# A four-column exponential moved later in ScalarE's order, in an attention and feed-forward kernel

## The chip, the cores and the metric

The kernel runs on one core of a Trainium2 chip. The metric is the device time of one launch in microseconds; smaller is better.

## What is computed

The input x has 8 batches of 1024 rows and 256 columns, in fp32. Cut to what matters, the reference is:

```python
q, k, v = x @ Wq.T + bq, x @ Wk.T + bk, x @ Wv.T + bv      # split into 16 heads of 16
q = softmax(q, axis=-1)                                    # over a head's 16 columns
k = softmax(k, axis=-2)                                    # over the batch's 1024 rows
state = einsum('bhnd,bhne->bhde', k, v)                    # 16 x 16 per head
out = einsum('bhnd,bhde->bhne', q, state)                  # back to (8, 1024, 256)
x = layernorm(x + layernorm(out) @ Wo.T + bo)

h = gelu(layernorm(x) @ ternary(w1).T + b1)                # 1024 hidden columns
x = layernorm(x + layernorm(h) @ ternary(w2).T + b2)
```

The keys' softmax is over all rows of a batch, and the kernel treats a batch in two blocks. Each block takes its own maximum of the keys; at the end the two blocks have to be weighed against each other with the exponential of (block's maximum minus the larger maximum). That weight is the subject of the change.

## The kernel before

**Blocks.** The 8 batches of 1024 rows are 16 blocks of 512 rows (`blocks`, two for each batch: g = 0 and g = 1; so odd blocks have g = 1). A block is 4 tiles of 128 rows.

**The order is written out by hand.** `ORDER` is a table of strings. The main loop takes i from 0 to 20 and reads one string for each i: "early" for the first four, "mid" for 4 to 15, and strings of their own for the five at the end. Each word of a string is a piece, and `piece(what, i)` issues it. One pass of a string works on several blocks at once: queries and keys of block i, attention of an earlier block, and the feed-forward part (`H`, `A`, `B`) of a still earlier one. Each engine executes its own instructions in the order in which the pieces issue them and waits on semaphores for the others.

**Work that is dealt out in between.** VectorE's small work (norms, statistics, residual sums) is written as generators. They lie in the queues `soon`, `behind` and `later`, and `more(n)` takes n steps from them; the words `m`, `m1` to `m8` are calls of it.

**The pieces beside the change:**

- `k0`, `k1`, `kb`, `ke`: the keys. `keys_exp` is two exponentials of 128x512 on ScalarE (L383), with the block's maximum as bias; the block's sum goes to `z[b]`.
- `bs`: `blocks_sum(b)`, in odd blocks only. VectorE takes the maximum of the two blocks' maxima (L460, `m`), after one step of dealt-out work subtracts it (L463, `e`, 128x4), and ScalarE takes the exponential in place (L466).
- `te0`, `te2`: `turn_keys`, TensorE transposes of the keys, copied by ScalarE to `ek` (L400).
- `a`: `attend`, matmuls to `po` (L545), copied by ScalarE to `o` and `y` (L550, L551); VectorE takes statistics of `o` (L555, L557).
- `qe`, `qs`: the queries' exponential on ScalarE (L428, 128x1024), their sums and reciprocals on VectorE (L433, L435), and the product on GpSimd (L436).
- `bw`: `blocks_weights(b)`, in odd blocks only: four small VectorE instructions (L471, L473, L475, L477) that turn `e` into the two weights. The first of them needs the exponential.
- `cr`: in odd blocks the weights are used: `first_block` on ScalarE (L482) and `second_block` on VectorE (L489). Then a DMA adds the row `crow` to x (L991).
- `A`, `B`: `product`, the second matmul of the feed-forward part (L726) into PSUM `pf`; when a half is done ScalarE copies it to `zs[i]` (L739, called z in the profile), a tile with one buffer. `rest(i)` reads it on VectorE (L798, L803) to update x.
- `en`: `enter`, a GpSimd product to `h0` (L614) and a DMA (L617). `ti0`, `ti1`: its transposes (`pth`), copied by ScalarE and VectorE (L635, L636).
- `sh`, `sq`: `sum_halves` and `sum_squares`: a DMA that adds two halves (L699), and TensorE's transposes of the sum (`psq`, L711).

The name z stands for two things in the profile: `zs[i]` of L739 and L798, and the small sums of L471 and L473.

Of the kernel before, what the change touches and what calls it, by code (L numbers as in the profile page):

```python
# [11 lines left out]
AF = mybir.ActivationFunctionType  # L12
# [13 lines left out]
def attn_ffn_postln_kernel(  # L26
# [11 lines left out]
    nc = tc.nc  # L38
    B, N, C = x.shape
# [283 lines left out]
    es, mb, z, mx, a0, aT, sT, sm = {}, {}, {}, {}, {}, {}, {}, {}  # L323
# [133 lines left out]
    def blocks_sum(b):  # L457

        m = small.tile([P, KC], F32, tag="m", name=f"m_{b}")
        nc.vector.tensor_tensor(m, mb[b][:, 0, :], mb[b][:, 1, :], ALU.max)  # L460
        e = small.tile([P, NB, KC], F32, tag="e", name=f"e_{b}")
        more(1)
        nc.vector.tensor_tensor(  # L463
            e, mb[b], m.unsqueeze(1).to_broadcast([P, NB, KC]), ALU.subtract
        )
        nc.scalar.activation(e, e, AF.Exp)  # L466
        es[b] = e, m

    def blocks_weights(b):
        e, m = es[b]  # L470
        nc.vector.tensor_tensor(z[b], z[b], e, ALU.mult)  # L471
        more(1)
        nc.vector.tensor_tensor(m, z[b][:, 0, :], z[b][:, 1, :], ALU.add)  # L473
        more(1)
        nc.vector.reciprocal(m, m)  # L475
        more(1)
        nc.vector.tensor_tensor(e, e, m.unsqueeze(1).to_broadcast([P, NB, KC]), ALU.mult)  # L477
# [127 lines left out]
    h0, hT, ph, u, sq, sqs, sums, sn, pf, mv, rs, sc, ms, zs = ({} for _ in range(14))  # L605
# [75 lines left out]
    def lower(n):  # L681

        i, j = n // HC, n % HC
        if upper_on_vector(n):
            nc.vector.tensor_scalar(u[n][:, 0, :], ph[n], gm[:, j : j + 1], None, ALU.mult)
        nc.vector.scalar_tensor_tensor(  # L686
            u[n][:, 1, :], ph[n], gm[:, j : j + 1], u[n][:, 0, :].bitcast(F32),
            ALU.mult, ALU.subtract,
        )
        if j % 2 == 1 and 1 < j < (HC if i < len(blocks) - 1 else HC - 2):  # L690
            nc.gpsimd.dma_start(sums[i], sq[i], accum_op=ALU.add)  # L691
# [166 lines left out]
    def more(n):  # L858

        for _ in range(n):  # L860
            done = False
            for queue in (soon, behind, later):
                while queue and not done:
                    steps, wait = queue[0]
                    if wait > 0:
                        break
                    wait = next(steps, soon)
                    if wait is soon:
                        queue.pop(0)
                        continue  # L870
                    queue[0][1] = wait or 0
                    done = True
                if done:
                    break
            passed()
# [6 lines left out]
    def apply(n):  # L882

        for _ in range(n):
            if applies:
                _, x_t, sh, rs = applies.pop(0)
                nc.scalar.activation(x_t, x_t, AF.Identity, bias=sh, scale=rs)
# [6 lines left out]
    ORDER = {  # L894
        "early": """
            tx0/ph m3 m q0 m3 q2 m2 st0/ph m1 qm k0 st1/tp m2 p p k1 p st2/ph tq0/pf kb m2 st3/tp
            m tq1/w ke bs a/pf m4 m2 a/w te0/pf te2/ph m m1 p m p p p en m3 tx1/w m4 m4 x0 qe m
            bw qs a/w m6 a/w ti0/ph x1 m4 m2 cr ti1/ph m p m
        """,
        "mid": """  # L900
            H m6 H m q0 q2 m1 m2 m3 m st0/tp qm m6 H st1/tp sq/w H p m k0 p k1 p kb p m3 H H A m8
            A A st2/w m1 H A tq0/tp H m3 A st3/w A ke p tx0 A bs m m4 m2 a/ph A m4 m a/w tq1/ph
            a/w te0 p B te2/w qe p tx1/w p B B en B bw qs x0 ti1/ph p m4 m a/w x1 m4 B cr m1 m3
            ti0/ph B m2 m3 B m m2 p p B sh
        """,
        "16": """
# [23 lines left out]
    def turn(what, n, parts=1):  # L930

        k = count[what]
        count[what] += k < n * parts
        return (k // parts, k % parts) if k < n * parts else None
# [3 lines left out]
    def piece(what, i):  # L938
        NBL, CHUNKS = len(blocks), len(blocks) * HC
        real = i < NBL  # L940
        b, g = i // NB, i % NB
        state = g == 0 and 0 < b <= B
        if what == "H":
            one = turn("H", CHUNKS)
            if one:
                assert count["ti"] >= (one[0] // HC + 1) * KC
                hidden(one[0])
                if low:
                    lower(low.pop())
                low.append(one[0])  # L950
        elif low:
            lower(low.pop())
        if what in ("A", "B"):
            one = turn(what, CHUNKS)
            if one:
                product(one[0], "AB".index(what))
        elif what[0] == "m":
            more(int(what[1:] or 4))
            next(prep, None)
        elif what == "p":  # L960
            apply(1)
        elif what in ("q0", "q2") and real:
            queries(i, int(what[1]))
        elif what == "qm" and real:
            queries_max(i)
        elif what == "qe" and real:
            queries_exp(i)
        elif what == "qs" and real:
            queries_sum(i)
        elif what in ("k0", "k1") and real:  # L970
            keys(i, int(what[1]))
        elif what == "kb" and real:
            keys_bias(i)
        elif what == "ke" and real:
            keys_exp(i)
        elif what == "bs" and real and g == 1:
            blocks_sum(b)
        elif what == "bw" and real and g == 1:
            blocks_weights(b)
        elif what in ("te0", "te2") and real:  # L980
            turn_keys(i, int(what[2]))
        elif what in ("x0", "x1") and real:
            keys_x(i, int(what[1]))
        elif what == "cr" and real:
            if g == 0:
                a0[b] = big.tile([P, KC, C], F32, tag="a0", bufs=2, name=f"a0_{b}")
                nc.scalar.copy(a0[b], pa[i])
            else:
                first_block(b)
                second_block(b)  # L990
            nc.gpsimd.dma_start(  # L991
                x_of(i), crow.unsqueeze(1).to_broadcast([P, G, C]), accum_op=ALU.add
            )
        elif what in ("tx0", "tx1"):
            turn_x(i + 1, int(what[2]))
        elif what[:2] == "tq" and i > 0:
            one = turn("tq", NBL, KC)
            if one:
                turn_queries(*one)
        elif what == "st0" and state:  # L1000
            state_turn(b - 1)
        elif what == "st1" and state:
            state_values(b - 1)
        elif what in ("st2", "st3") and state:
            state_out(b - 1, int(what[2]) - 2)
        elif what == "a" and i > 1:
            one = turn("a", NBL, G)
            if one:
                assert count["tq"] >= (one[0] + 1) * KC
                attend(*one)  # L1010
                if one[1] == G - 1:
                    (behind if one[0] > NBL - 3 else later).append([norm(one[0]), 0])
        elif what == "en" and i > 2:
            one = turn("en", NBL)
            if one:
                while one[0] not in normed:
                    more(1)
                while any(a[0] <= one[0] for a in applies):
                    apply(1)
                enter(one[0])  # L1020
        elif what[:2] == "ti" and i > 2:
            one = turn("ti", NBL, KC)
            if one:
                n = one[0]
                assert count["en"] > n and count["H"] >= (n if n < NBL - 2 else 0) * HC
                turn_input(*one)
        elif what == "sh" and i > 3:
            one = turn("sh", NBL)
            if one:
                n = one[0]  # L1030
                assert count["H"] - len(low) >= n * HC + (HC if n < NBL - 1 else HC - 1)
                sum_halves(n)
        elif what == "sr" and i > last:
            if turn("sr", 1):
                assert count["sh"] == NBL and count["H"] - len(low) == CHUNKS
                add_squares(NBL - 1, sqs[CHUNKS - 1])
        elif what == "sq" and i > 4:
            one = turn("sq", NBL)
            if one:
                n = one[0]  # L1040
                assert count["sh"] > n and (n < NBL - 1 or count["sr"])
                sum_squares(n)
                if n < NBL - 1:
                    assert count["B"] >= (n + 1) * HC
                    behind.append([rest(n, (0, G)), 0])
# [3 lines left out]
    for i in range(last + 5):  # L1049
        names = {last + k: str(16 + k) for k in range(5)}  # L1050
        for what in ORDER[names.get(i, "early" if i < 4 else "mid")].split():
            what, _, tag = what.partition("/")
# [48 lines left out]
```

## Time and profile before

| what | value |
|---|---|
| median of 3 runs | 682.49 us (680.82 to 683.73) |
| profiled execution, its own time | 683.59 us |
| its span | 681.9 us |
| TensorE, matmuls | 610.2 us busy, 89% |
| VectorE | 521.1 us busy, 76% |
| ScalarE | 497.9 us busy, 73% |
| GpSimd | 298.9 us busy, 44% |
| exponential L466 | 8 instructions of 205 ns |

A profile line reads: start and duration in us, engine, line of the kernel, operation, output <- input, size; in brackets the idle time of that engine just before it and who ended it. PE is TensorE, DVE is VectorE, ACT is ScalarE, POOL is GpSimd. In the table of groups a row ends with the busy time of the group, the mean duration in ns, and the idle time ahead of it with what ended it.

### The profile page before, as it was taken

Reading aid. Unit: us, or ns where it says so; the run is one execution under the profiler, and the core shown is the slowest. Engines: PE = TensorE matmul, PEld = TensorE weight load, DVE = VectorE, ACT = ScalarE, POOL = GpSimd, SP = SyncE. Lnnn points to the kernel's source line nnn. Section 1 sums busy time; section 2 is a strip of 40 time slices with the busy share of each in tenths; the row PEclk is TensorE's granted clock in tenths of the full one; section 3 lists DMA queues with packets and bytes.
Section 4 is the critical chain, followed back from the end, with each engine's and each line's share of the span. In section 5 each row is a group of like instructions: output and inputs, shape, how many; then the busy total and the mean of one; then the engine's idle time right before and its main releaser. Section 6 shows DMA issues by size and latency. Waiting matters only on the chain.

```text
span 681.9 us, 9515 instructions
## 1 busy us (share of the span) xinstructions
PE 610.2 (89%) x3200; PEld 480.1 (70%) x3200; DVE 521.1 (76%) x1453; ACT 497.9 (73%) x936; POOL 298.9 (44%) x265
## 2 busy tenths in 40 slices
PE   5899989999999899999999899999999889977860
PEld 3567657877777687767778687777777677766750
DVE  1566776488978787788878887788878888867886
ACT  3544388797887879687887879697887878777820
POOL 1212443533454635544453635545444633562432
PEclk9889999999999999999999999999999999987985
DMA  8522242445464563547373653545463544365621
GB/s 295 192 31 32 31 62 51 78 75 93 66 151 63 124 108 82 114 69 154 62 163 55 126 106 87 112 70 120 74 128 47 126 74 110 62 108 125 139 62 62
DMA packets 34466, 66.31 MB, mean 97 GB/s; under 512 B 3408, under 2 KB 21840, under 8 KB 34416
## 3 DMA queue, kind: packets, MB, share of 16 engines
q0 software_dynamic: 25904, 45.49, 39.7%
q1 hardware_dynamic: 8240, 19.94, 7.8%
q8 instruction: 25, 0.41, 0.2%
q10 hardware_dynamic: 272, 0.26, 0.1%
q14 instruction: 25, 0.20, 0.1%
HBM read 11.95 MB, written 8.39 MB: 30 GB/s over the span
## 4 chain that ended last, share of the span: by engine, by line
PE 54%; DVE 22%; ACT 14%; issue 4%; DMA 3%; POOL 2%; SPq 0%; ACTq 0%; POOLq 0%; DVEq 0%
PE ph L659 10%; PE pf L726 9%; PE pk L363 8%; PE pa L452 7%; PE pq L409 7%; DVE x L798 5%; PE po L545 4%; ACT sq L649 4%; DVE x L803 4%; ACT ph L665 4%; DVE u L686 4%; DMA sums<-sums 2%; ACT u L668 2%; PE pth L631 2%; PE ptx L342 1%
## 5 line engine op out<-in xcount | busy, mean ns | idle before, releaser
L726 PE MATMUL pf<-t,u 128*128 128x258 f32 x1024 | 164.6, 299 | 20.6 <-ACT z L739 15.9
L726 PEld LDWEIGHTS pf<-t,u 128*128 128x128 f32 x1024 | 140.9, 192 | 37.1 <-ACT z L739 18.7
L659 PE MATMUL ph<-hT,t 128*128 128x512 f32 x512 | 149.9, 423 | 11.9 <-DVE u L686 7.6
L686 DVE SCALAR_TENSOR_TENSOR u<-ph,gm,u 128x512 fp32r<-128x512 f32 x128 | 95.4, 748 | 53.8 <-ACT sq L649 48.5
L659 PEld LDWEIGHTS ph<-hT,t 128*128 128x128 f32 x512 | 91.8, 192 | 39.1 <-DVE u L686 13.8
L665 ACT ACTIVATE ph<-ph,bh 128x512 f32<-128x512 f32 x128 | 85.0, 664 | 23.0 <-PE ph L659 21.2
L545 PE MATMUL po<-sm,qT 128*128 128x384 f32 x256 | 92.9, 488 | 0.0
L668 ACT ACTIVATE u<-ph,gm 128x512 fp32r<-128x512 f32 x120 | 82.5, 688 | 3.9
L436 POOL TENSOR_TENSOR q<-q,rq 128x1024 f32<-128x1024 f32 x16 | 31.0, 1940 | 101.7 <-DVE rq L435 101.7
L691 POOL DMA_DIRECT2D sums<-sq x47 | 42.6, 905 | 73.9 <-DMA sums<-sq 21.1
L649 ACT ACTIVATE sq<-ph,shift 128x512 f32<-128x512 f32 x96 | 65.3, 681 | 0.2
L452 PE MATMUL pa<-x,ek 128*128 128x256 f32 x256 | 61.5, 384 | 0.2 <-ACT ek L400 0.2
L144 POOL TENSOR_TENSOR ny_y<-nvy,mhalf 128x8 f32<-128x8 f32 x16 | 26.5, 1657 | 77.6 <-DVE nvy L584 77.6
L409 PE MATMUL pq<-wqkv_sb,xT 128*128 128x256 f32 x256 | 59.8, 387 | 0.0
L363 PE MATMUL pk<-xT,wqkv_sb 128*128 128x512 f32 x128 | 58.0, 593 | 0.4 <-DVE q L413 0.4
L545 PEld LDWEIGHTS po<-sm,qT 128*128 128x128 f32 x256 | 43.8, 190 | 20.0 <-ACT sm L532 2.9
L452 PEld LDWEIGHTS pa<-x,ek 128*128 128x128 f32 x256 | 48.2, 193 | 9.6 <-ACT ek L400 0.6
L409 PEld LDWEIGHTS pq<-wqkv_sb,xT 128*128 128x128 f32 x256 | 49.2, 194 | 8.0 <-issue 0.9
L423 POOL TENSOR_TENSOR q<-q,qm 128x1024 f32<-128x1024 f32 x16 | 30.9, 1933 | 53.5 <-DVE qm L422 51.4
L798 DVE SCALAR_TENSOR_TENSOR x<-z,sc,x 128x256 f32<-128x256 f32 x60 | 45.8, 763 | 0.0
L363 PEld LDWEIGHTS pk<-xT,wqkv_sb 128*128 128x128 f32 x128 | 24.0, 190 | 24.5 <-issue 20.3
L635 ACT ACTIVATE hT<-pth,gs 128x512 fp32r<-128x512 f32 x32 | 21.9, 688 | 26.1 <-PE pth L631 26.1
(169 smaller groups left out, 1135.9 us busy)
## 6 DMA issues: line engine op xcount, KB each, us to landing
sums<-sq POOLq DMA_DIRECT2D x47, 512.0 KB, 4.6
x<-in_x_dram SPq DMA_DIRECT2D x16, 512.0 KB, 6.6
x<-crow POOLq DMA_DIRECT2D x16, 512.0 KB, 5.5
x<-bout POOLq DMA_DIRECT2D x16, 512.0 KB, 5.6
out_dram<-x SPq DMA_DIRECT2D x15, 512.0 KB, 2.7
sums<-sums POOLq DMA_DIRECT2D x15, 256.0 KB, 6.0
w<-in_w_dram SPq DMA_DIRECT2D x4, 512.0 KB, 7.7
wqkv_sb<-in_wqkv_dram SPq DMA_DIRECT2D x2, 256.0 KB, 6.5
```

What stands on the lines that cost most here:

```text
L363: nc.tensor.matmul(pk, wqkv_sb[:, k, C + c * P : C + (c + 1) * P], xT[i][:, k, :], start=(k == 0), stop=(k == KC - 1),)
L409: nc.tensor.matmul(pq[:, n, :], xT[i][:, k, (t + n) * P : (t + n + 1) * P], wqkv_sb[:, k, 0:C], start=(k == 0), stop=(k == KC - 1),)
L452: nc.tensor.matmul(pa[i][:, c, :], ek[i][:, t, c * P : (c + 1) * P], x_of(i)[:, t, :], start=(t == 0), stop=(t == G - 1),)
L545: nc.tensor.matmul(po[:, c * P : c * P + P + C], qT[i][:, c, t * P : (t + 1) * P], sm[b][:, c, :], start=(c == 0), stop=(c == KC - 1), ski ...
L649: nc.scalar.activation(sqs[n], ph[n], AF.Square, bias=shift)
L659: nc.tensor.matmul(ph[n], t1[:, k, j * P : (j + 1) * P], hT[i][s][:, k, :], start=(s == 0 and k == 0), stop=(s == 1 and k == KC - 1),)
L665: nc.scalar.activation(ph[n], ph[n], AF.Gelu, bias=bh[:, j : j + 1])
L668: nc.scalar.activation(u[n][:, 0, :], ph[n], AF.Copy, scale=gm[:, j : j + 1])
L686: nc.vector.scalar_tensor_tensor(u[n][:, 1, :], ph[n], gm[:, j : j + 1], u[n][:, 0, :].bitcast(F32), ALU.mult, ALU.subtract,)
L691: nc.gpsimd.dma_start(sums[i], sq[i], accum_op=ALU.add)
L726: nc.tensor.matmul(pf[i, m][t], u[n][:, s, (2 * m + t) * P : (2 * m + t + 1) * P], t2[:, j, :], start=(j == 0 and s == 0), stop=(j == HC - ...
L798: nc.vector.scalar_tensor_tensor(x_t, outputs(i, t)[:, :C], sc[i][:, t : t + 1], x_t, ALU.mult, ALU.add)
```

## The change

The exponential is taken out of `blocks_sum` and becomes a piece of its own, `be`, with a function `blocks_exp`. In the two strings that hold odd blocks with `bs`, the word `be` stands just ahead of `qe`. `blocks_sum` keeps its two VectorE instructions where they were, and stores `es[b]` for the later pieces as before. In "mid" fourteen words lie between `bs` and `be`.

```diff
         nc.vector.tensor_tensor(
             e, mb[b], m.unsqueeze(1).to_broadcast([P, NB, KC]), ALU.subtract
         )
-        nc.scalar.activation(e, e, AF.Exp)
         es[b] = e, m
+
+    def blocks_exp(b):
+        nc.scalar.activation(es[b][0], es[b][0], AF.Exp)
...
     ORDER = {
         "early": """
...
-            m tq1/w ke bs a/pf m4 m2 a/w te0/pf te2/ph m m1 p m p p p en m3 tx1/w m4 m4 x0 qe m
+            m tq1/w ke bs a/pf m4 m2 a/w te0/pf te2/ph m m1 p m p p p en m3 tx1/w m4 m4 x0 be qe m
...
         "mid": """
...
             A A st2/w m1 H A tq0/tp H m3 A st3/w A ke p tx0 A bs m m4 m2 a/ph A m4 m a/w tq1/ph
-            a/w te0 p B te2/w qe p tx1/w p B B en B bw qs x0 ti1/ph p m4 m a/w x1 m4 B cr m1 m3
+            a/w te0 p B te2/w be qe p tx1/w p B B en B bw qs x0 ti1/ph p m4 m a/w x1 m4 B cr m1 m3
...
+        elif what == "be" and real and g == 1:
+            blocks_exp(b)
```

## Prediction

> **What bounds the kernel now.** I read the page's busy shares first, then the chain that ended last, then the groups, and then the order of events around one of the moved exponentials.
>
> ```profile
> PE 610.2 (89%) x3200; PEld 480.1 (70%) x3200; DVE 521.1 (76%) x1453; ACT 497.9 (73%) x936; POOL 298.9 (44%) x265
> ...
> PE 54%; DVE 22%; ACT 14%; issue 4%; DMA 3%; POOL 2%; SPq 0%; ACTq 0%; POOLq 0%; DVEq 0%
> ```
>
> TensorE is busy for 89% of the span and holds 54% of the chain; VectorE holds 22%, ScalarE 14%. Shortening ScalarE alone therefore pays only where TensorE really waits for it. Two rows of the groups (all rows, shapes apart) say where ScalarE stands idle near the change:
>
> ```profile
> L739 ACT COPY z<-pf 128x258 f32<-128x258 f32 x60 | 19.5, 381 | 19.8 <-DVE x L798 13.7 <-PE pf L726 6.0
> L466 ACT ACTIVATE e<-e 128x4 f32<-128x4 f32 x8 | 1.6, 205 | 12.2 <-DVE e L463 12.2
> ```
>
> The moved exponential (L466, eight of them, 205 ns each) has 12.2 us of idle ScalarE in front of it, all for VectorE's subtraction at L463. That is the prize on offer. Whether it can be cashed depends on what stands behind it, so here is the timeline round the sixth of the seven waits, every engine, with rows left out:
>
> ```profile
> 464.05 2.41 DVE L460 TENSOR_TENSOR m<-mb 128x2 f32<-128x2 f32 x1
> 464.23 2.20 POOL L614 TENSOR_TENSOR h<-x,rs_all 128x1024 f32<-128x1024 f32 x1
> ...
> 466.78 0.15 DVE L463 TENSOR_TENSOR e<-mb,m 128x4 f32<-128x4 f32 x1
> ...
> 466.96 0.21 ACT L466 ACTIVATE e<-e 128x4 f32<-128x4 f32 x1 [1.69 <-DVE e L463]
> 467.07 0.35 ACT L550 COPY o<-po 128x256 f32<-128x256 f32 x1
> 467.29 0.48 DVE L798 SCALAR_TENSOR_TENSOR x<-z,sc,x 128x256 f32<-128x256 f32 x1
> 467.32 0.38 ACT L551 COPY y<-po 128x256 f32<-128x256 f32 x1
> ...
> 467.86 0.65 ACT L739 COPY z<-pf 128x258 f32<-128x258 f32 x2 [0.16 <-DVE x L798]
> ...
> 468.29 0.79 PE L726 MATMUL pf<-t,u 128*128 128x258 f32 x4 [1.33 <-ACT z L739]
> ```
>
> TensorE waits 1.33 us for the copies of z. They stand third behind the exponential, but they have a second condition: z has one buffer, so they may not start before VectorE has read the previous block's z with the last L798 (467.29 + 0.48 = 467.77). They start at 467.86, 0.09 us after it. The even blocks have no such exponential and show what is left without it:
>
> ```profile
> 351.83 0.39 ACT L550 COPY o<-po 128x256 f32<-128x256 f32 x1
> 352.09 0.40 ACT L551 COPY y<-po 128x256 f32<-128x256 f32 x1
> ...
> 353.72 0.48 DVE L798 SCALAR_TENSOR_TENSOR x<-z,sc,x 128x256 f32<-128x256 f32 x1
> ...
> 354.29 0.65 ACT L739 COPY z<-pf 128x258 f32<-128x258 f32 x2 [1.79 <-DVE x L798]
> ```
>
> There the same o and y copies run early, z still waits 1.79 us for L798, and it again starts 0.09 us after L798's end. So this wait of TensorE belongs to VectorE.
>
> **What the Trainium skill says.** "PSUM — Partial Sum Buffer", section "Engine vs sequencer instructions": ScalarE's, VectorE's and GpSimd's queues are strict FIFO. The trace agrees: the o copy at 467.07 goes 0.11 us after the exponential's start, though its own matmuls on TensorE had ended by 464.79 (the L545 group that starts at 463.34 and takes 1.45). "SBUF — State Buffer", section "Who interferes with whom": a VectorE instruction with two SBUF inputs blocks against a GpSimd instruction that reads SBUF. The trace agrees: L460 on two columns takes 2.41 us beside GpSimd's L614, where the same instruction takes 0.15 at 314.02, clear of L614. This is what makes L463 late. "ScalarE: Activation LUTs", section "What ACT_TABLE_LOAD costs": back-to-back ACTIVATEs overlap by about 93 ns, and a table load is 1283 ns for each switch of set. The trace shows 1283 ns for each of its 26 loads, and 0.11 us as the exponential's net time on the queue.
>
> **The change part by part.** The order of the instructions on each engine shows that only ScalarE's order moves. TensorE, VectorE, GpSimd and SP keep theirs, DMA issues and table loads included: the moved piece issues one instruction and no DMA. In "mid" it goes past the o and y copies, the z copies, qT, two more o and y, and the two ek copies, and lands in front of the queries' exponential.
>
> (a) *The wait that is taken away.* Six sites in "mid": 1.99 + 1.97 + 1.85 + 1.90 + 1.69 + 2.34 = 11.74 us of idle ScalarE; with 0.42 at the first site that is the 12.2. Without the wait the first o and y copies start about 1.7 us sooner, at 465.3 when the xT copy of 464.69 ends. The z copies stay at L798 + 0.09. What is late next is z itself: its 0.16 us of waiting becomes about 1.8, as in the even blocks. TensorE's next matmul stays at 468.29. Gain for TensorE: 0.
>
> (b) *The exponential in its new place.* From the z copies on ScalarE runs without a gap to the queries' exponential (467.86 to 472.04), so the later work shifts by 0.11 us at each site: L428 from 470.88 to 470.99, and the xT copy behind it from 471.84 to 471.95. ScalarE then stands idle 1.07 us for TensorE's pth, which swallows it. Cost: 0.
>
> (c) *The new wait.* VectorE's L471 (z times e) runs at 470.74, ahead of the new exponential: that starts at about 470.88 and ends at 471.08, so L471 starts at 471.12, 0.38 us late, and VectorE's queue stands behind it: two statistics pairs, L473, L475, L477, then the queries' sum L433. L433 ran at 472.06 and was released by the queries' exponential at about the same moment, so it goes to 472.44 and the reciprocal L435 ends at 474.25 instead of 473.87. Next is L636, which already waits 0.43 us for ScalarE's hT and starts at 474.30: the 0.38 is gone there. On GpSimd, L436 starts 0.38 later and ends at 476.33; L564 on VectorE and GpSimd's L144 follow it, so L144 goes from 476.20 to about 476.43, and the crow and sums DMAs behind it (L991, L699) by the same 0.23. VectorE's L146 comes at about 477.7, still ahead of L636's start at 478.23. The sums transfer is used by TensorE's transposes 8.19 us after L699's start (478.03 to 486.22); the slowest landing of its 15 is 7.4 us, so 0.8 us is spare and 0.23 is used. Cost: 0 at each of five sites alike. The last site (546.85) already has L435 ending where L636 starts, so there some 0.3 us slips, to be swallowed by 0.23 at L555, 0.23 at L489 and 0.50 at the second L636. No trace of before shows this wait. Bounds: if nothing absorbed it, 6 x 0.38 = +2.3; on the other side, if shifted DMAs spared TensorE the waits for sums that it has in two even blocks, -(0.41 + 0.69) = -1.1. I take 0.
>
> (d) *The two "early" sites.* At 47.7 the exponential's wait (0.42) stands before ek copies that wait for TensorE anyway; at the new place L471 (53.48) is long after it. At 86.49 there is no wait, the chain runs through ScalarE, and the exponential's 0.09 us leaves the part ahead of ek and returns ahead of L428. VectorE's L471 goes from 88.09 to about 91.2, but behind it VectorE was idle 3.35 us for that same L428. Together -0.1 at most.
>
> Sum: 0 + 0 + 0 - 0.1 = -0.1 us. The profiled execution had 683.59 us, of which 681.9 are the span; the median of the three runs is 682.49, 1.1 below it. The shift applies to either: **682.4**. With the bounds of (c) this case alone lies between 681.0 and 684.8. The three runs shown spread over 0.43%, and 0.5% (3.4 us) is about what a measurement of this kernel can tell from no change.
>
> **Rivals.** *Faster: ScalarE's order is what holds TensorE at z.* Then the six waits of TensorE for z at these sites (1.37 + 1.61 + 1.49 + 1.54 + 1.33 + 1.50 = 8.84 us) go: 673.7, and half of it is 678.1. For it: 12.2 us of idle time before L466, and TensorE does stop for z each time. Against it: the 0.09 us between L798's end and z in both kinds of block. Smaller routes to it are earlier free PSUM banks from o and y.
>
> *Slower: the late exponential delays the sums add-on.* L471 holds VectorE, L435 releases L436 late, and L699 stands behind L436 in GpSimd's queue. It decides once L699 slips by more than the spare 0.8 us of (c), or its landing grows by that as it meets other transfers; TensorE then stops at the psq transposes, as in two even blocks, 0.41 and 0.69 us. At six sites 6 x 0.69 = +4.1: 686.6. For it: slacks of 0.43 and 0.8 are thin and transfers vary. Against it: the computed slip is 0.23.
>
> *The change doesn't do what it says*, that is, the wait stays in front of o because another condition holds it: then 682.5, within the first case.
>
> **How the numbers follow.** First case 0.58, faster rival 0.24, slower rival 0.18. The two rivals get that much because the site repeats six times: an error of 0.6 us in one of them is enough to leave the band of 3.4 us. Range 677.0 to 687.0: it holds the first case, the slower rival up to its price, and the third of the faster one that gains least. Chances: faster 0.24, same 0.58, slower 0.18.
>
> **What would show it.** Right: the idle time before L466 drops from 12.2 us to near 0, that of L739 behind L798 rises from 13.7 to about 24, TensorE's wait for z stays near 15.9, and a new VectorE wait at z (L471 before) of about 0.4 us appears at six sites. Wrong: z starting before L798's end plus 0.09, TensorE's wait for z falling by several us, the psq transposes waiting in odd blocks, or the odd blocks' length (37.0 to 38.3 us between the 12-matmul pieces of pf) moving by more than 0.4 us.

## The result, and the profile after

The kernel after takes 684.72 us (median of 9 runs, 683.99 to 686.36), the kernel before 682.49 us (9 runs, 680.82 to 684.03). The ratio is 1.0036, with a 95% interval of 1.002 to 1.0052: slower by 2.2 us. The forecast was no change. 684.72 lies inside the range of the prediction, and at the edge of what it states for its first case (681.0 to 684.8), but that is luck: the upper end there was six "mid" waits that nothing absorbs, and the loss was made elsewhere, as the runs below show. The profiled execution of after had 684.28 us, of which 682.6 are the span.

The page of the kernel after, busy shares and the chain that ended last by engine, shows next to nothing of it:

```profile
PE 609.7 (89%) x3200; PEld 478.2 (70%) x3200; DVE 524.1 (77%) x1453; ACT 497.5 (73%) x936; POOL 299.0 (44%) x265
...
PE 51%; DVE 23%; ACT 15%; issue 5%; DMA 3%; POOL 2%; SPq 0%; ACTq 0%; POOLq 0%; DVEq 0%
```

The groups of after, shapes apart (busy us, mean ns, idle time ahead and its releasers), show that the change did what it says. The exponential, now L469, waits for nothing any more, and the z copies wait longer for VectorE instead (26.4 us, 13.7 before):

```profile
L741 ACT COPY z<-pf 128x258 f32<-128x258 f32 x60 | 19.5, 380 | 32.4 <-DVE x L800 26.4 <-PE pf L728 6.0
L469 ACT ACTIVATE e<-e 128x4 f32<-128x4 f32 x8 | 2.2, 281 | 0.0
```

The waits (sum in us, number, longest) show what that is worth. Before:

```profile
PE pf L726 <- ACT z L739: 15.9, 12, 1.7
```

After, with one line that was not expected:

```profile
PE pf L728 <- ACT z L741: 15.7, 12, 1.7
...
DVE z L473 <- ACT e L469: 5.4, 7, 3.1
```

TensorE still waits 15.7 us for z (15.9 before). VectorE waits 5.4 us for the exponential in its new place, and of these 3.1 are a single wait. The timeline of after at the site that the prediction showed looks as predicted, with rows left out:

```profile
467.91 0.15 DVE L463 TENSOR_TENSOR e<-mb,m 128x4 f32<-128x4 f32 x1
...
468.43 0.48 DVE L800 SCALAR_TENSOR_TENSOR x<-z,sc,x 128x256 f32<-128x256 f32 x1
...
469.00 0.65 ACT L741 COPY z<-pf 128x258 f32<-128x258 f32 x2 [2.02 <-DVE x L800]
...
469.42 0.79 PE L728 MATMUL pf<-t,u 128*128 128x258 f32 x4 [1.31 <-ACT z L741]
...
472.35 0.16 DVE L473 TENSOR_TENSOR z<-z,e 128x4 f32<-128x4 f32 x1 [0.39 <-ACT e L469]
```

z starts 0.09 us after L800's end (468.91), TensorE waits 1.31 us where it waited 1.33, and VectorE's new wait is 0.39. So the loss is not here. To find it, I cut both executions at the start of the queries' exponentials (L428), one for each i:

| stretch | before, us | after, us | difference |
|---|---|---|---|
| start of the span to i = 3 | 91.02 | 89.87 | -1.15 |
| i = 3 to 4 | 35.88 | 38.19 | +2.31 |
| i = 4 to 15, eleven blocks | 420.09 | 420.36 | +0.27 |
| i = 15 to the end of the span | 134.88 | 134.14 | -0.74 |

The eleven "mid" blocks are unchanged. The first row is not the change: 1.08 of its 1.15 us are there at the exponential of i = 1 (50.90 before, 49.82 after), and the granted clock of TensorE up to there had a mean of 0.93 before, with two stretches of 3.4 us at half speed, and 1.00 after. e8 below, which has the order of before and in its profile no such stretch, is there at 49.41. In the last row the mean clock was 0.88 before and 0.90 after. So the two profiled spans differ by 0.7 us where the medians differ by 2.2. What is left is i = 3, the second "early" site. Its timeline before, rows left out:

```profile
88.09 0.13 DVE L471 TENSOR_TENSOR z<-z,e 128x4 f32<-128x4 f32 x1
...
90.77 1.89 POOL L614 TENSOR_TENSOR h<-x,rs_all 128x1024 f32<-128x1024 f32 x1 [5.93 <-ACT x L887]
...
91.02 1.11 ACT L428 ACTIVATE q<-q 128x1024 f32<-128x1024 f32 x1
...
92.16 1.22 DVE L433 TENSOR_REDUCE rq<-q 128x64 f32<-128x1024 f32 x1 [3.35 <-ACT q L428]
...
97.80 1.44 PE L659 MATMUL ph<-hT,t 128*128 128x512 f32 x5 [0.75 <-DVE hT L636]
...
100.21 3.70 PE L409 MATMUL pq<-wqkv_sb,xT 128*128 128x256 f32 x16
```

The same place in the timeline of after:

```profile
89.52 1.89 POOL L616 TENSOR_TENSOR h<-x,rs_all 128x1024 f32<-128x1024 f32 x1 [5.85 <-ACT x L889]
89.76 0.26 ACT L469 ACTIVATE e<-e 128x4 f32<-128x4 f32 x1
89.87 1.10 ACT L428 ACTIVATE q<-q 128x1024 f32<-128x1024 f32 x1
...
90.06 1.37 DVE L473 TENSOR_TENSOR z<-z,e 128x4 f32<-128x4 f32 x1 [3.14 <-ACT e L469]
...
91.94 1.21 DVE L433 TENSOR_REDUCE rq<-q 128x64 f32<-128x1024 f32 x1
...
97.34 1.43 PE L661 MATMUL ph<-hT,t 128*128 128x512 f32 x5 [1.45 <-DVE hT L638]
...
99.95 5.09 PE L409 MATMUL pq<-wqkv_sb,xT 128*128 128x256 f32 x16
```

Read it from L473. It was done at 88.22, long before GpSimd's product to h0. Now it starts inside that product (89.52 to 91.41) and takes 1.37 us instead of 0.13, ending as the product ends. Three small instructions and the queries' sum L433 stand behind it: L433 starts 2.07 us after the exponential's start instead of 1.14. VectorE passes the delay on to hT (L638), and TensorE's last five ph matmuls start 7.47 us after the exponential instead of 6.78. The chain that ended last runs through this place in both executions (start, time on the chain; rows left out). Before:

```profile
91.17 0.97 ACT q L428
...
92.16 1.23 DVE rq L433
...
97.09 0.67 DVE hT L636
...
97.80 0.51 PE ph L659
```

After:

```profile
89.92 0.11 ACT e L469
...
90.06 1.38 DVE z L473
...
92.02 1.14 DVE rq L433
...
96.63 0.67 DVE hT L638
...
97.34 0.51 PE ph L661
```

Then something else is seen. The sixteen pq matmuls (L409) take 5.09 us instead of 3.70. The windows view shows the clock (stretch, length, busy time and count of PE, PEld, DVE, ACT and POOL, then the granted TensorE clock, the DMA share and GB/s). After:

```profile
99.95:101.00 1.05, 1.05 (x4) 0.87 (x5) 0.98 (x4) 0.74 (x2) 0.00 (x0) 0.50 1.19 174
101.00:102.00 1.00, 1.00 (x4) 0.82 (x3) 0.96 (x4) 0.00 (x0) 0.00 (x0) 0.50 1.05 151
```

Before, at its pq matmuls:

```profile
99.95:101.00 1.05, 1.04 (x6) 0.96 (x7) 1.02 (x4) 1.02 (x2) 0.00 (x0) 1.00 1.18 175
```

From 99.36 to 102.77 the clock of after is at half speed, for 3.4 us, behind a stretch of equal length in which TensorE was busy for 1.43 us.

### The profile page after: what moved, and what is told of

Same layout as the page of the kernel before. It is cut to its first block, busy times and chain, and to the rows that moved or that the text cites. A ratio compares the mean times of both kernels' runs of the same rounds, so it can differ in the third digit from the quotient of the medians.

```text
span 682.6 us, 9516 instructions
## 1 busy us (share of the span) xinstructions
PE 609.7 (89%) x3200; PEld 478.2 (70%) x3200; DVE 524.1 (77%) x1453; ACT 497.5 (73%) x936; POOL 299.0 (44%) x265
## 4 chain that ended last, share of the span: by engine, by line
PE 51%; DVE 23%; ACT 15%; issue 5%; DMA 3%; POOL 2%; SPq 0%; ACTq 0%; POOLq 0%; DVEq 0%
PE ph L661 10%; PE pf L728 8%; PE pk L363 7%; PE pq L409 7%; PE pa L452 7%; DVE x L800 5%; ACT sq L651 4%; PE po L547 4%; DVE x L805 4%; DVE u L688 4%; ACT ph L667 4%; ACT u L670 2%; PE pth L633 2%; DMA sums<-sq 1%; DMA x<-in_x_dram 1%
## 5 line engine op out<-in xcount | busy, mean ns | idle before, releaser
L728 PE MATMUL pf<-t,u 128*128 128x258 f32 x1024 | 164.9, 299 | 20.9 <-ACT z L741 15.7
L409 PE MATMUL pq<-wqkv_sb,xT 128*128 128x256 f32 x256 | 60.7, 391 | 0.0
L409 PEld LDWEIGHTS pq<-wqkv_sb,xT 128*128 128x128 f32 x256 | 49.9, 197 | 8.6 <-issue 1.2
L800 DVE SCALAR_TENSOR_TENSOR x<-z,sc,x 128x256 f32<-128x256 f32 x60 | 43.4, 723 | 0.0
L741 ACT COPY z<-pf 128x258 f32<-128x258 f32 x60 | 19.5, 380 | 32.4 <-DVE x L800 26.4
```

The lines of the kernel that those rows point to most:

```text
L409: nc.tensor.matmul(pq[:, n, :], xT[i][:, k, (t + n) * P : (t + n + 1) * P], wqkv_sb[:, k, 0:C], start=(k == 0), stop=(k == KC - 1),)
L728: nc.tensor.matmul(pf[i, m][t], u[n][:, s, (2 * m + t) * P : (2 * m + t + 1) * P], t2[:, j, :], start=(j == 0 and s == 0), stop=(j == HC - ...
L800: nc.vector.scalar_tensor_tensor(x_t, outputs(i, t)[:, :C], sc[i][:, t : t + 1], x_t, ALU.mult, ALU.add)
```

## The experiments

The theories: the loss is made at i = 3 by the product that holds L473 (A); TensorE's half clock adds to it (E). Against them stand the small delays at the six mid sites (B), a place that is too late for VectorE whatever runs beside it (C), and a cost of the exponential's place by some other way (D). All times are medians; kernels that were measured in one group share the runs of before.

| run | median us (runs) | before, us (runs) | ratio, 95% |
|---|---|---|---|
| e1, moved in mid alone | 683.22 (22) | 682.27 (59) | 1.0006, 0.9987 to 1.0024 |
| e2, moved in early alone | 684.80 (22) | 682.27 | 1.0029, 1.0009 to 1.0049 |
| e3, earlier in early | 683.18 (14) | 682.27 | 1.0006, 0.9986 to 1.0027 |
| e4, product in four | 682.85 (14) | 682.27 | 0.9997, 0.9977 to 1.0017 |
| e5, before with a hold | 684.74 (22) | 683.27 (60) | 1.0019, 1.0002 to 1.0036 |
| e6, weights behind the sums | 687.86 (7) | 683.27 | 1.0067, 1.0044 to 1.009 |
| e7, after with extra matmuls | 682.72 (22) | 683.27 | 0.9993, 0.9977 to 1.0009 |
| e8, before with extra matmuls | 682.30 (22) | 683.27 | 0.9989, 0.9972 to 1.0006 |
| e9, before with a late product | 665.04 (6) | 681.48 (11) | 0.9736, 0.9702 to 0.977 |
| e10, after with a late product | 667.33 (6) | 681.48 | 0.9775, 0.9745 to 0.9804 |
| e11, e9 with two short matmuls | 664.27 (6) | 683.55 (11) | 0.9724, 0.9692 to 0.9757 |

**e1 and e2: one string at a time.** Against after, e1 takes `be` out of "early", e2 out of "mid"; the piece `bs` then issues the exponential itself:

```diff
         elif what == "bs" and real and g == 1:
             blocks_sum(b)
+            if i < 4:          # e2: i >= 4
+                blocks_exp(b)
```

> The exponential stands ahead of the queries' exponential at the six sites of "mid" only; at the two sites of "early" it stands where it did before. Theory A (the one site at i = 3 costs everything: VectorE's L473 there falls beside GpSimd's product L616): no loss, 682.5 us give or take 0.7, ratio 0.999 to 1.001. Rival B (the six sites of "mid" cost 0.38 us each, unabsorbed): all of the loss, 684.7, ratio 1.0036. In the profile by A: pieces of the chain in "mid" as long as before, L473 late by 0.4 us at six sites with nothing after it late.

> The other half of the change: moved at the two sites of "early" only. Theory A: all of the loss, 684.7 us, ratio 1.0025 to 1.0045, with L473 at i = 3 taking over 1 us beside GpSimd's product. Rival B: no loss, 682.5, ratio 0.999 to 1.001.

Six moved exponentials alone give a ratio whose interval holds 1; two alone give the loss. L473 at i = 3 in the timeline of e1:

```profile
88.89 0.13 DVE L473 TENSOR_TENSOR z<-z,e 128x4 f32<-128x4 f32 x1
```

and in that of e2:

```profile
90.18 1.38 DVE L473 TENSOR_TENSOR z<-z,e 128x4 f32<-128x4 f32 x1 [3.14 <-ACT e L469]
```

Compared with each other, the 22 runs of e2 have a mean 1.4 us above that of the 22 of e1 (95% interval 0.2 to 2.6). So the early sites make the loss, and the six mid sites none that can be measured. From i = 3 to 4 e2 takes 39.78 us; it has two half-clock stretches there in a row (6.8 us). But e1 takes 37.62 there, without any hold: it also shows one stretch of 3.4 us. So the half clock at this place is not made by the hold alone.

**e3: the move kept, but short.** In "early", `be` stands behind `te2/ph`, some pieces ahead of `qe`:

```diff
-  ... te0/pf te2/ph m m1 p m p p p en m3 tx1/w m4 m4 x0 be qe m
+  ... te0/pf te2/ph be m m1 p m p p p en m3 tx1/w m4 m4 x0 qe m
```

> As the changed kernel, but in "early" the exponential stands right behind the copies of ek, ahead of ScalarE's four normalisations of x, which release GpSimd's product. Theory A: L473 runs near 87.5 us, before the product starts, in 0.13 us; no loss, 682.5 us, ratio 0.999 to 1.001. Rival C (any place behind the o, y and ek copies is too late for VectorE at i = 3[...]): most of the loss stays, 684 or more. Rival B: 684.7.

The timeline of e3 has L473 clear of the product, which starts at 90.02:

```profile
88.03 0.17 DVE L473 TENSOR_TENSOR z<-z,e 128x4 f32<-128x4 f32 x1 [0.71 <-ACT e L469]
```

The ratio is 1.0006, and i = 3 to 4 takes 35.94 us (35.88 before). A wait of 0.71 us for the exponential costs nothing that can be measured; it is the place beside the product that costs. Against e2, of the same group, e3 gains 1.7 us in the mean (interval 0.5 to 2.9).

**e4: the move kept, the product cut.** The exponential stands where after has it, but the first product to h0 is four instructions of 128x256:

```diff
-        nc.gpsimd.tensor_tensor(
-            h0[i], x_of(i), rs2.unsqueeze(2).to_broadcast([P, G, C]), ALU.mult
-        )
+        parts = range(G) if i == 0 else (slice(None),)
+        for t in parts:
...
+            nc.gpsimd.tensor_tensor(
+                h0[i][:, s, :], x_of(i)[:, s, :],
...
```

> As the changed kernel, but GpSimd's first product h0 (128x1024, 1.89 us) is cut into four of 128x256 with the same result. Theory A[...]: L473 at i = 3 is held by one quarter at most, so it takes 0.6 us or less instead of 1.37, and 0.5 to 0.8 us of the loss come back (684.0), less some tenths if four products take longer than one. If the 1.37 us has another cause, L473 stays at 1.3 or more. The half-clock window after it may go or stay.

The timeline of e4:

```profile
88.21 2.33 POOL L620 TENSOR_TENSOR h<-x,rs_all 128x256 f32<-128x256 f32 x4 [4.39 <-ACT x L894]
...
90.20 0.35 DVE L473 TENSOR_TENSOR z<-z,e 128x4 f32<-128x4 f32 x1 [3.15 <-ACT e L469]
```

The products now start as their rows are ready and end at 90.54, and L473 ends at 90.55. It has the same wait for the exponential as in after (3.15 us), but is held for 0.35 us, and the loss is gone (0.9997; 35.68 us from i = 3 to 4), 2.1 us below e2 in the mean (1.0 to 3.2) and more than the 0.5 to 0.8 us that were expected back. By itself e4 would leave a rival, as h0 is also done a microsecond sooner (0.52 us after the start of L428, 1.54 in after); in e3 it is not (1.65, and 1.64 in before). e3 and e4 undo the hold in two ways that have nothing else in common. This, with e5, is what shows A.

**e5: the hold without the move.** The kernel before, with an unused reduction on VectorE ahead of the queries' sum at i = 3:

```diff
+        if i == 3:
+            nc.vector.tensor_reduce(idle[:, 0:48], heads(i)[:, 0:48, :], AX.X, ALU.add)
```

> The kernel before, with the exponential where it was, and one more VectorE instruction at i = 3 only: a sum over 48 of the 64 heads of q, right ahead of L433, its output unused; about 0.9 us. Theory A (what costs is VectorE arriving about 0.9 us late at L433 at i = 3, whatever holds it): the same loss as the changed kernel, 683.9 to 685, and the distance of the queries' exponentials at i = 3 and i = 4 grows from 35.9 to 36.4 or more. Rival D (the place of the exponential costs by some other way): no loss, 682.3.

The timeline of e5:

```profile
92.36 0.95 DVE L435 TENSOR_REDUCE idle<-q 128x48 f32<-128x768 f32 x1 [3.35 <-ACT q L428]
...
98.63 1.42 PE L662 MATMUL ph<-hT,t 128*128 128x512 f32 x5 [1.38 <-DVE hT L639]
```

0.95 us at this one place give TensorE the wait of after (1.38; after 1.45, before 0.75) and the loss, 1.0019 with an interval just clear of 1, with two half-clock stretches behind it (39.65 us from i = 3 to 4). A delay of VectorE there is enough; no exponential has to move.

**e6: a mend that failed.** In "early", the weights go behind the queries' sums, so that L473 cannot hold L433:

```diff
-            bw qs a/w m6 ...
+            qs bw a/w m6 ...
```

> The changed kernel, but in "early" the words bw and qs change places, so that VectorE's L473 to L479 stand behind the sum and the reciprocal of the queries. The exponential stays late. Theory A: L473 no longer holds L433 and runs after GpSimd's product, so most of the loss goes: 682.3 to 683.0, distance i = 3 to i = 4 35.9 to 36.3 where TensorE's clock is full. Rival C (late weights cost by their users on ScalarE, L484): the loss stays, 684 or more.

This was expected to gain, and lost 4.6 us. The timeline of e6:

```profile
93.67 2.06 POOL L436 TENSOR_TENSOR q<-q,rq 128x1024 f32<-128x1024 f32 x1
...
93.96 1.79 DVE L479 TENSOR_TENSOR e<-e,m 128x4 f32<-128x4 f32 x1
...
95.85 0.91 ACT L484 ACTIVATE a<-a,e 128x256 f32<-128x256 f32 x2 [2.19 <-DVE e L479]
```

The last of the four weight instructions now falls beside GpSimd's next long instruction, the queries' product. It takes 1.79 us instead of 0.16, and ScalarE waits 2.19 us for the weights. The hold was moved, not removed. The same happens at i = 1: there L479 takes 1.64 us beside that product (0.16 in after), and i = 1 to 2 takes 19.31 us (18.14 before, 18.04 in after).

**e7 and e8: TensorE kept busy.** To after (e7) and to before (e8) three extra matmuls of 128x512 on constant data are added in the two gaps of TensorE at i = 3; nothing reads their result.

```diff
+                if n == 0 and s == 1 and k == KC - 1:
+                    keep_awake(2)
...
+            keep_awake(1)
```

> The changed kernel with three matmuls of 128x512 more, whose output is unused, in the waits of TensorE at the first block of the hidden layer (two ahead of the last matmul of its first piece, one ahead of the shift's sum), near 97 and 99 us. Theory E (the stall makes a window of half TensorE clock near 100 us likelier, which doubles its price): no half-clock window near 100 us in the profile, and 683.0 to 683.6. If the loss is the stall alone, or the extra work costs as much as it saves: 684.5 to 685.

> The kernel before with the same three matmuls. Theory E: the window near 100 us comes in some executions of the kernel before too, so this gains a little, 681.5 to 682.3, and lies 0.5 to 1.0 us under the changed kernel with the same matmuls. If the window is no matter: 682.3 to 682.7.

In neither profile does the clock fall near 100 us, and i = 3 to 4 takes 36.83 us in e7 and 36.85 in e8: the loss of after is gone, though L473 in e7 still takes 1.37 us. By E, e8 was to lie 0.5 to 1.0 us under e7; the medians are 0.4 apart, and the means 0.1 the other way. The extra matmuls are too large for the gap: the first group takes 1.88 us on TensorE, and fills in e7 the very wait that the hold makes. So these two go with a full clock in one execution each, and don't separate the hold from it. Both intervals hold 1.

**e9, e10 and e11: the product made to wait.** If a long GpSimd product costs so much beside one small instruction, what does it cost in the mid blocks? Before, one VectorE instruction with two SBUF inputs takes 2.4 to 3.0 us beside it in each of the eleven: L460 in two blocks (2.41 us in the one that the prediction showed), L798 in seven, L803 in two. In e9 (on before) and e10 (on after) GpSimd first copies one column of the last residual update of VectorE, and so starts its product behind all of them:

```diff
+        if last_x:
+            nc.gpsimd.tensor_copy(mark, last_x.pop())
         nc.gpsimd.tensor_tensor(h0[i], x_of(i), ...)
...
+            last_x[:] = [x_t[:, 0:1]]      # in rest, behind the update L803
```

> The kernel before, with a copy of one column on GpSimd ahead of each product of h0 in "mid", which makes that product wait for VectorE's last L803 of the residual sums; so it no longer runs beside the instructions with two SBUF inputs. [...]those instructions take 0.15 and 0.48 us, z is copied some 2 us sooner, TensorE's waits for z (15.9 us in all) go, and ScalarE's wait for e (12.2 us) falls below 4: 667 to 674 us. If the hold has another cause, or the later product makes TensorE wait at its transposes instead: 682 or more.

> The same on the changed kernel. Theory A: the site at i = 3 is untouched (its product has no residual sums to wait for), so the loss of about 2 us against e9 stays, 669 to 676. If the place of the exponential has a cost or a gain in "mid" once VectorE no longer holds z, the two differ by more than 3 us, or the moved one is faster.

The timeline of e9 in the block of the sixth wait:

```profile
454.00 0.15 DVE L460 TENSOR_TENSOR m<-mb 128x2 f32<-128x2 f32 x1
...
456.06 0.18 POOL L618 COPY mark<-x 128x1 f32<-128x1 f32 x1 [1.61 <-DVE x L808]
456.21 1.89 POOL L619 TENSOR_TENSOR h<-x,rs_all 128x1024 f32<-128x1024 f32 x1
```

and its z copies in the groups, shapes apart:

```profile
L744 ACT COPY z<-pf 128x258 f32<-128x258 f32 x60 | 19.8, 394 | 10.5 <-PE pf L731 6.0 <-DVE x L803 4.4
```

The wait of TensorE for z in e9 (15.9 us before):

```profile
PE pf L731 <- ACT z L744: 1.7, 1, 1.7
```

L460 takes 0.15 us, no L803 or L808 takes more than 0.73, z waits 4.4 us for VectorE instead of 13.7, and the wait of TensorE for z falls from 15.9 to 1.7. e9 is 2.6% faster than before. Together with after, where the exponential's wait went and the wait for z stayed, this shows that VectorE's residual updates set the pace at z, as part (a) of the prediction had it. The median of e10 lies 2.3 us above that of e9, with L473 held at i = 3 as in after:

```profile
90.10 1.38 DVE L473 TENSOR_TENSOR z<-z,e 128x4 f32<-128x4 f32 x1 [3.14 <-ACT e L469]
```

That is the size of the loss, but with six runs of each the intervals of the two ratios overlap, so it is not shown that the move costs the same here.

e11 is e9 with two matmuls of 128x256 in the gaps at i = 3 (0.59 us each in its timeline), short enough to fit:

```diff
+        pd = ps.tile([P, TB], F32, tag="tp", bufs=1, name="pd")
+        nc.tensor.matmul(pd[:, 0:C], ones, wqkv_sb[:, 0, 0:C], start=True, stop=True)
```

> e9 (exponential where it was before, GpSimd's product late) with two matmuls of 128x256 more in TensorE's two waits near 97 and 99 us, output unused; each about 0.5 us, so that they fit into waits of 0.75 us. Theory E: no half-clock window near 100 us, and up to 1.7 us of e9 saved in the executions that have it: 664.0 to 665.2. If so little work does not hold the clock, or other windows move: 665 to 666.

i = 3 to 4 takes 35.88 us without a half-clock stretch, where the profiled e9 took 37.59 with one. In the medians this is not told apart from e9: 0.9724 against 0.9736, with intervals that overlap. Its 664.27 us are the lowest median here.

**What the half clock costs.** One execution of each kernel is in the traces. The time from i = 3 to 4:

| hold at i = 3 | half clock behind it | executions |
|---|---|---|
| no | none | before 35.88, e3 35.94, e4 35.68, e11 35.88 |
| no | 3.4 us | e1 37.62, e9 37.59 |
| yes | 3.4 us | after 38.19 |
| yes | 6.8 us | e2 39.78, e5 39.65, e6 (held at L479) 40.36, e10 39.84 |

One stretch costs 1.7 us here (37.62 - 35.88), the hold itself 0.6 (38.19 - 37.62): estimates from one execution each. The 0.6 fits the 0.69 us by which TensorE's five ph matmuls start later in after. Without extra matmuls all five executions with a hold show the half clock, and two of the five without one (before, e1, e3, e4 and e9).

Every timed run has its mean granted clock too; a straight line through the runs, with a constant for each kernel, gives about 0.95 us for each 3.4 us at half clock, wherever it falls. Compared at the same clock, before has 682.6 to 683.1 us in the different groups, e1 682.8, e3 682.6, e4 682.2, and e2 684.2, e5 684.15, after 684.05; e7 has 682.9 and e8 683.1. The standard errors are 0.1 to 0.35. What these runs do not show is that the hold lowers the mean clock: it is 0.9746 in e2, and 0.9747 in e1, e3 and e4 of the same group, which have no hold. One stretch is worth 0.0025 of it, so that up to 0.8 of a stretch more or less would not be seen.

**What stays open.** How often the clock falls at i = 3 in each kernel is known from single executions. At the same clock 1.1 to 1.4 us remain, more than the 0.6 that the cut shows. A stretch that costs 1.7 here where the mean is 0.95 could explain most of the rest, but no run shows that, and the mean clocks neither show nor exclude it.

## Why the prediction was wrong, point by point

**(a), the wait that is taken away: right.** Gain 0 was said. The exponential's idle time went from 12.2 us to 0, that of z behind VectorE rose to 26.4 (about 24 was said), and TensorE waits 15.7 us for z. The faster rival fell with it; e9 shows what does move z.

**(b), the new place: right.** The eleven mid blocks together moved by 0.27 us.

**(c), the new wait: right.** VectorE's wait is 0.25 to 0.40 us at the six mid sites (0.38 was said), the 0.43 us of waiting at hT that was to swallow it is gone, and e1 measures no loss. The slower rival is not what happened: its place was the transposes of the sums (psq), which have 8.2 us of idle time ahead of them before and 8.5 after. The bounds of this part, put together as the prediction gives them, are 681.3 to 684.7, not 681.0 to 684.8; nothing hangs on that.

**(d), the two early sites: wrong.** The step read: L471 goes "to about 91.2, but behind it VectorE was idle 3.35 us for that same L428". Two things are wrong with it. The start was right in kind (the instruction comes with the exponential), but its duration was carried over from its old place. At the new one GpSimd's product runs, as the profile before already showed: it stood at 90.77 and took 1.89 us. The prediction had quoted the Trainium skill ("SBUF — State Buffer", section "Who interferes with whom") for just this case, a VectorE instruction with two SBUF inputs against a GpSimd instruction that reads SBUF, and had shown it at L460. It was not applied to the instruction that the change moves. The runs agree with that section: 1.37 us in after, 1.38 in e2, 0.35 in e4, 0.13 to 0.17 away from the product. And the 3.35 us of idle time lay ahead of L433, so they hide what comes before its releaser, not what ends after it: L433 was released at about 92.1 in before, and only what passes that instant counts. Worked out from the same rows: the product ends at 92.66, the three small instructions behind L471 take about 0.5 with their gaps, so L433 starts at about 93.15 instead of 92.16. That is +1.0 us on the chain that ended last, which already ran from L428 to L433; 0.93 was measured at L433. At i = 1 the step was right: from i = 1 to 3 there are 40.12 us before and 40.05 after.

**A term that no step had.** The sum added delays of TensorE one to one. At i = 3 the clock makes more of them. The Trainium skill, "TensorE: Matmul & The Clock Gate", section "Part 1: The HAM clock gate", describes a clock of two speeds, set by how busy TensorE was in a free-running window of 3413 ns. The trace agrees with the two values (0.50 and 1.00) and with the length (3.4 and 6.8 us). The page puts the fall behind an idle window; here it came behind windows in which TensorE was busy for 1.43 of 3.41 us (after) and 1.92 (e1), with no gap over 1.45 us, so the measurement decides. Nor does the busy time of the window ahead decide it. The window of e1 ahead of its fall, and the window of before at the same matmuls, counted on from the fall of before at 24.99 us in 22 steps of that length (windows view as above, e1 first):

```profile
97.77:101.18 3.41, 1.92 (x9) 1.27 (x9) 3.24 (x10) 2.60 (x6) 1.73 (x2) 1.00 0.71 104
96.67:100.08 3.41, 1.93 (x8) 0.98 (x7) 3.24 (x11) 2.60 (x6) 2.02 (x2) 1.00 0.71 105
```

The first was followed by half speed, the second was not; and before fell to half speed at 35.23 us, behind a window in which TensorE was busy for 3.41 of 3.41 us. The page's free-running window would let the same kernel fall in one execution and not in another, as before and e8 do ahead of i = 1, but no run shows that its phase is the cause.

So the step that failed is the duration of L471 in its new place, 0.13 us carried over where 1.37 were measured, and with it the 3.35 us of idle time that were to cover it. That this hold makes the loss is shown. Of the 2.2 us, 0.6 are the delay itself by the cut. The half clock behind it, in all five profiled executions with a hold and two of five without, is a candidate for the rest, and that part stays open.

## What to carry to other kernels

When an instruction is moved, price it in its new company: look up what the other engines run at the new time, and for a VectorE instruction with two SBUF inputs look for a long GpSimd instruction first. A moved instruction's consumers move too, and the one site of a different kind deserves its own timeline, however many equal sites there are. Idle time hides a delay only up to the moment at which it would have ended.

## What the runs showed of the hardware that was not expected

Delaying a GpSimd product of 128x1024 by about the length of VectorE's residual updates made the kernel faster by 2.6% (681.48 to 665.04 us): the updates of 128x256 with two SBUF inputs (L798) went from a mean of 763 ns to 482, and VectorE's busy time from 521.1 to 494.7 us.

TensorE's clock fell to half for a stretch of 3.4 us though no gap of TensorE in the 3.4 us ahead was longer than 1.45 us, and one such stretch over dense matmuls cost 1.7 us (e1 against before, one execution each). In one profiled execution (e11) two unneeded matmuls of 0.59 us in the gaps went with a full clock there, at no cost in the time from i = 3 to 4 (35.88 us).
